# Starting the first attention's steps after 512 of 2048 tokens, with the rest of the token work among its first twelve steps

## The chip, the cores and the metric

The kernel runs on one core of a Trainium2 chip. The metric is device microseconds from launch to end; the kernel before takes 1487.89 us, the median of three runs (1487.07 to 1488.57). Five engines run side by side, each through its own instruction queue in order: PE (matrix multiply, with weight loads shown as PEld), DVE (vector), ACT (scalar), POOL (GpSimd) and SP, which issues most of the DMAs. Engines wait for each other through semaphores.

## The reference, cut to what matters

Two layers over x of 2048 tokens by 128. The change touches the first attention of the first layer only. It has 16 heads of 8 dimensions, and its weights are relu(scores) over their sum:

```python
xn = _layernorm(x, axis=-1)
# first attention, on xn
qkv = (xn @ w_qkv).reshape(Bx, Sx, H, 3 * HD)
q, k, v = jnp.split(qkv, 3, axis=-1)          # each to (B, H, S, HD), HD = 8
scores = jnp.einsum('bhqd,bhkd->bhqk', q, k) / sqrt(HD)
w = relu(scores)
attn = w / (jnp.sum(w, axis=-1, keepdims=True) + KERN_EPS)
out = jnp.einsum('bhqk,bhkd->bhqd', attn, v)
out = out.transpose(0, 2, 1, 3).reshape(Bx, Sx, D) @ w_out + b_out
y = xn + out
s = (y - mean(y)) * rsqrt(var(y) + LN_EPS) * gamma + beta
g = silu(routed_block(xn))                     # ranks tokens by a router, treats 255 of them
x = x + s * g                                  # then the second layer
```

## The kernel before, in words

**Program order.** PE, ACT and DVE run in the order in which the program is written (a manual schedule); POOL's and SP's instructions are put in order by a planner that follows dependencies and priorities.

**Prelude.** `begin()` (L795) runs before the attention's steps. The 2048 tokens are four blocks of 512. For each, the generator `normalised(i)` (L764) works in two halves: first statistics (L774 to L777: four BN pairs and a sum on DVE, a square root on ACT), then the reciprocal and four small DVE operations (L779 to L783), four DVE normalisations into `xne` (L785), four PE transposes (L101) and an ACT copy into `xnT` (L103). `keys(i)` (L712) projects block i onto group 0's keys and `queries()` (L721) block 0 onto group 0's queries. Both go through `project` (L700): one matmul of 512 columns, an ACT copy that rounds the result to `high` (fp32r), and a DVE operation (L709) that leaves in each row either the high part or the difference, by the per-partition scalars `low_k` and `low_q` (L137). `values(i)` (L752) makes the values of four 128-token chunks. All four blocks go through all of it before the first step.

**Rows.** fp32 scores are made from two fp32r parts of each operand: a quadrant of 32 partitions holds one head, with four variants (high or low key by high or low query) of its 8 dimensions. Before, the variant is the outer index (rows n*8 + d); `low_k` tests bit 16 and `low_q` bit 8 of the partition number.

**Steps.** 256 steps (L964): 4 query chunks of 512, by 4 groups of 4 heads, by 16 key chunks of 128. `scores(n)` (L818) is four matmuls (L824), one for each head, in four quadrants at once, each into a PSUM bank of tag "s" (6 banks), then four relus, on ACT (L832) or DVE (L834) by the running totals `work.a` and `work.d` (`Work.lesser`, L189). `products` (L837) of two steps earlier is four matmuls (L840) into one accumulator, copied by ACT at the end of a group (`group_out`, L847). After these, a step either does the piece that `due` lists for it, or takes one turn of `others()`: the routed block (router, ranking, its own small attention), then weights and the gated output of finished chunks. The routed block and `spread` share the one PSUM bank of tag "x".

**Other groups' keys and queries.** `all_keys(i)` (L746) and `all_queries(qc)` (L749) project all 16 heads of a block at once through `spread` (L724): a matmul, an ACT copy to `high` (two buffers), a DVE subtraction to `low`, and four stores into DRAM in the order of the variants. `group` (L741) loads 128 rows back with one DMA into `kT` or `qT`. `due` has all_queries(0) at step 1, all_keys(0 to 3) at steps 4, 8, 12 and 16, and the other query chunks at 40, 104 and 168. `read` has the loads of groups 1 to 3.

**The routed block's start.** `routed_block` (L217) loads its weights, sets up constants on POOL (L245 to L271) and yields once; that first turn is taken before `begin()` (L695).

Of the kernel before, what the change touches and what calls it, by code (L numbers as in the profile page):

```python
# [11 lines left out]
F32 = mybir.dt.float32  # L12
# [5 lines left out]
ALU = mybir.AluOpType  # L18
# [4 lines left out]
P = 128  # L23
# [3 lines left out]
NQ = S // 512  # L27
H = 16
HD0 = 8
G = 4  # L30
# [75 lines left out]
def layer0(ctx, tc, a, small, ident, xin, xn1T, row_load, second):  # L106
    nc = tc.nc

    ends, steps, block = ExitStack(), ExitStack(), ExitStack()
    ps = steps.enter_context(tc.tile_pool(name="l0_ps", bufs=1, space=PSUM))  # L110
    dram = ctx.enter_context(tc.tile_pool(name="rb_dram", bufs=2, space=DRAM))
    end = ends.enter_context(tc.tile_pool(name="l0_end", bufs=1, side="right"))
    keep = steps.enter_context(tc.tile_pool(name="l0", bufs=1))


    aw = steps.enter_context(tc.tile_pool(name="aw", bufs=2))
    w_qkv = aw.tile([P, 512], F32, tag="high", name="w_qkv")[:, : 3 * D].rearrange(
        "p (g j t d) -> p g j t d", g=G, j=4, t=3
    )
    nc.scalar.dma_start(  # L120
        out=w_qkv.rearrange("p g j t d -> p (g j t d)"), in_=a["w_qkv"]
    )

    w_k = keep.tile([P, 4, 4, HD0], F32, name="w_k")
    w_q = keep.tile([P, 4, 4, HD0], F32, name="w_q")
    for i in range(4):
        for t, dst in ((1, w_k), (0, w_q)):
            nc.gpsimd.tensor_copy(dst[:, :, i, :], w_qkv[:, 0, :, t, :])
    w_ka = keep.tile([P, H, HD0], F32, name="w_ka")
    w_qa = keep.tile([P, H, HD0], F32, name="w_qa")  # L130
    for t, dst in ((1, w_ka), (0, w_qa)):
# [85 lines left out]
def routed_block(  # L217
# [3 lines left out]
    nc = tc.nc  # L221
# [8 lines left out]
    for t, n in enumerate(("wq", "wk", "wv")):  # L230
# [9 lines left out]
    pos = rb.tile([P, NC], I32, name="r_pos")  # L240
    nc.sync.dma_start(out=pos, in_=a["pos"])


    tok = rb.tile([P, 512], F32, name="tok")
    nc.gpsimd.iota(  # L245
# [6 lines left out]
        out=before, in_=before, pattern=[[-1, P]], compare_op=ALU.is_gt,  # L252
# [12 lines left out]
    nc.gpsimd.tensor_copy(xne[:, :, 130], pos)  # L265

    qk = rb.tile([P, 2 * H, 32], F32, tag="qk_p4", name="qk")
    nc.gpsimd.memset(qk, 0.0)
    v = rb.tile([P, 2, H, 32], F32, name="r_v")
    nc.gpsimd.memset(v, 0.0)  # L270
    nc.gpsimd.memset(v[:, :, :, HD0 : HD0 + 1], 1.0)  # L271
# [408 lines left out]
def relu_attention(  # L680
# [3 lines left out]
    nc = tc.nc  # L684
# [12 lines left out]
    def bank(shape, tag="x"):  # L697
        return ps.tile(shape, F32, tag=tag, bufs=NS if tag == "s" else 1, name="t")

    def project(dst, w, i, low, tag="x"):  # L700

        t = bank([P, 512], tag)
        nc.tensor.matmul(
            t, w.rearrange("p b a d -> p (b a d)"), xnT[:, 512 * i : 512 * i + 512],
            start=True, stop=True,
        )
        high = aw.tile([P, 512], F32R, tag="high", name="high")
        nc.scalar.copy(high, t)
        nc.vector.scalar_tensor_tensor(dst, high, low, t, ALU.mult, ALU.add)  # L709
        work.add(a=0.6, d=0.75)  # L710

    def keys(i):  # L712
        project(kT[:, 0, 512 * i : 512 * i + 512], w_k, i, low_k, "s")

    qTs = {}

    def query_tile(qc, g):
        t = qTs[qc, g] = aw.tile([P, 512], F32R, tag="qT", bufs=3, name=f"qT_{qc}_{g}")
        return t

    def queries():  # L721
        project(query_tile(0, 0), w_q, 0, low_q, "s")

    def spread(w, i, order):  # L724


        t = bank([P, 512])
        nc.tensor.matmul(
            t, w.rearrange("p h d -> p (h d)"), xnT[:, 512 * i : 512 * i + 512],
            start=True, stop=True,  # L730
        )
        parts = [aw.tile([P, 512], F32R, tag=n, name=n) for n in ("high", "low")]
        nc.scalar.copy(parts[0], t)
        nc.vector.scalar_tensor_tensor(parts[1], parts[0], -1.0, t, ALU.mult, ALU.add)
        work.add(a=0.6, d=0.75)
        rows = dram.tile([G, 4, 4, HD0, 512], F32, tag="spread", bufs=8, name="spread")
        for n, x in enumerate(order):
            nc.sync.dma_start(out=rows[:, :, n, :, :], in_=parts[x].bitcast(F32))
        return rows

    def group(rows, g, dst):  # L741
        nc.sync.dma_start(out=dst.bitcast(F32), in_=rows[g].rearrange("j n d q -> (j n d) q"))

    asked, key_rows = {}, {}

    def all_keys(i):  # L746
        key_rows[i] = spread(w_ka, i, (0, 0, 1, 1))

    def all_queries(qc):  # L749
        asked[qc] = spread(w_qa, qc, (0, 1, 0, 1))  # L750

    def values(i):  # L752
        t = bank([P, 4, P], "s")
# [10 lines left out]
    def normalised(i):  # L764
# [27 lines left out]
        )  # L792
        yield

    def begin():  # L795
        parts = [normalised(i) for i in range(NQ)]
        next(parts[0])
        for i in range(NQ):
            if i + 1 < NQ:
                next(parts[i + 1])  # L800
            next(parts[i])
            if i:
                keys(i - 1)
            if i == 1:
                queries()
        values(0)
        keys(NQ - 1)
        for i in range(1, NQ):
            values(i)
        work.a = work.d = 0.0  # L810

# [126 lines left out]
        return [mv[:, i, 0:1] for i in range(n)], [r[:, i : i + 1] for i in range(n)]  # L938

    n_steps = NQ * G * NC  # L940
    due = {1: (all_queries, 0)}
    read = {}
    for i in range(NQ):
        due[4 + 4 * i] = (all_keys, i)
        for g in range(1, G):
            read[8 + 4 * i if g == 1 else 16 * g - 10 + 3 * i] = (g, i)
    for qc in range(1, NQ):
        due[64 * qc - 24] = (all_queries, qc)

# [9 lines left out]
            yield from gated(qc)  # L959

    ends, steps, block = pools
    ready, held, other = set(), [], others()
    begin()
    for n in range(n_steps + 2):  # L964
        if n < n_steps:
            held.append((n, scores(n)))
        if n >= 2:
            m, r = held.pop(0)
            products(m, r)
            if m % 16 == 15:  # L970
                group_out(m // 64, m // 16 % 4)
        if n in due:
            f, *args = due[n]
            f(*args)
        else:
            next(other)
        if n % 16 == 8 and 16 < n + 8 < n_steps:
            qc, g = (n + 8) // 64, (n + 8) // 16 % 4
            group(asked[qc], g, query_tile(qc, g))
# [746 lines left out]
```

## Time and profile before

| what | value |
|---|---|
| median of three runs | 1487.89 us |
| the profiled execution: its own time / its span | 1487.12 / 1485.1 us |
| busy, whole span: PE, DVE, ACT, POOL | 96%, 73%, 65%, 22% |
| mean granted clock of PE | 0.991 |
| first scores of step 0 start | 37.73 us |
| last scores of step 255 start | 500.92 us |
| relus: ACT 620 of mean 625 ns, DVE 404 of mean 684 ns | 326.3 and 261.2 us busy |

The profile is one execution. Busy times are sums over instructions; a span's rate is read better from the starts of successive instructions of one kind, since matmuls overlap in the pipeline. Scores of step n are recognised by L824, products by L840. Up to 37.7 us the engines go through the prelude; the steps follow to about 503 us, and the second layer after that.

### The profile page before, as it was taken

The numbers are of one execution on the slowest core, as the hardware profiler recorded it, in microseconds if no ns is written. First come the engines' busy times: TensorE is split into PE (matmuls) and PEld (weight loads), VectorE is DVE, ScalarE is ACT, GpSimd is POOL, SyncE is SP. The second block draws the span as 40 slices with busy tenths as digits, with TensorE's granted clock in tenths as the row PEclk, the third lists the DMA queues.
The fourth block names the chain that finished last, engine by engine and source line by source line (L and its number), as shares of the span: only waits on it lengthen the run. The fifth ranks groups of instructions, "written<-read, shape, count | busy, mean of one in ns | idle before, by whom it ended". The sixth has DMA issues, their size and how long they took to land.

```text
span 1485.1 us, 27124 instructions
## 1 busy us (share of the span) xinstructions
PE 1431.8 (96%) x10336; PEld 877.3 (59%) x10336; DVE 1079.6 (73%) x1938; ACT 967.2 (65%) x2080; POOL 325.2 (22%) x445
## 2 busy tenths in 40 slices
PE   4999999999999999999999999999999999999997
PEld 2223233332222367777777777777777777777775
DVE  5797878778888667567677667667767766777765
ACT  2787878778878656656556556556656655665663
POOL 1001000050000123322332242242242232252310
PEclk8999999999999999999999999999999999999999
DMA  2621100100200220000010010010001001000000
GB/s 66 186 66 61 32 12 14 49 26 14 60 20 4 79 50 15 15 16 15 21 24 15 15 30 15 15 29 15 15 15 29 15 15 29 15 15 16 15 22 22
DMA packets 28192, 44.70 MB, mean 30 GB/s; under 512 B 5984, under 2 KB 14560, under 8 KB 28064
## 3 DMA queue, kind: packets, MB, share of 16 engines
q1 hardware_dynamic: 27376, 41.94, 11.0%
q8 instruction: 81, 1.33, 0.4%
q0 software_dynamic: 256, 0.79, 0.2%
q14 instruction: 47, 0.39, 0.1%
q10 hardware_dynamic: 432, 0.26, 0.1%
HBM read 14.76 MB, written 10.11 MB: 17 GB/s over the span
## 4 chain that ended last, share of the span: by engine, by line
PE 60%; ACT 2%; DVE 1%; issue 1%; DVEq 0%; ACTq 0%
PE t L1326 18%; PE z L1376 17%; PE t L1556 16%; PE m L1436 2%; PE m L1264 2%; PE m L1229 2%; PE m L1279 2%; PE m L1421 2%; ACT p L1360 1%; ACT pt L1563 1%; PE m L1158 0%; DVE tops L1347 0%; PE m L1176 0%; DVE t L1346 0%; DVE pt L1563 0%
## 5 line engine op out<-in xcount | busy, mean ns | idle before, releaser
L1347 DVE TENSOR_REDUCE tops<-t 128x1 f32<-128x1024 f32 (+4 forms) x320 | 334.6, 1062 | 63.2 <-PE t L1326 56.0
L832 ACT ACTIVATE rt<-t 128x512 f32<-128x512 f32 x620 | 326.3, 625 | 76.1 <-PE t L824 75.0
L1563 ACT COPY pt<-t 128x512 f32<-128x512 f32 (+3 forms) x359 | 163.4, 518 | 266.9 <-PE t L1556 265.8
L1360 ACT ACTIVATE p<-t,tops 128x1024 f32<-128x1024 f32 (+7 forms) x384 | 331.2, 882 | 2.9 <-DVE tops L1347 2.2
L1326 PE MATMUL t<-k,q 128*128 128x512 f32 (+4 forms) x1280 | 316.6, 390 | 7.4 <-ACT p L1360 7.4
L834 DVE TENSOR_SCALAR rt<-t 128x512 f32<-128x512 f32 x404 | 261.2, 684 | 45.4 <-PE t L824 38.6
L840 PE MATMUL t<-rt,va 128*9 128x512 f32 x2048 | 270.3, 601 | 4.2 <-ACT part L856 3.8
L1556 PE MATMUL t<-ident,p 128*128 128x128 f32 x2176 | 270.1, 275 | 3.0 <-ACT x L1250 1.4
L1376 PE MATMUL z<-pt,v 128*64 128x256 f32 (+1 forms) x2304 | 268.3, 374 | 0.5 <-ACT zs L1570 0.5
L1326 PEld LDWEIGHTS t<-k,q 128*128 128x128 f32 x1280 | 218.6, 189 | 79.7 <-issue 36.1
L1556 PEld LDWEIGHTS t<-ident,p 128*128 128x128 f32 x2176 | 244.0, 141 | 25.5 <-ACT pt L1563 2.9
L1376 PEld LDWEIGHTS z<-pt,v 128*64 128x64 f32 x2304 | 151.6, 136 | 86.9 <-issue 21.4
L824 PEld LDWEIGHTS t<-qT,kT 32*128 32x128 f32 x1024 | 64.8, 183 | 189.0 <-ACT rt L832 112.9
L1563 DVE COPY pt<-t 128x512 f32<-128x512 f32 (+3 forms) x289 | 163.5, 605 | 2.6 <-PE z L1376 1.5
L824 PE MATMUL t<-qT,kT 32*128 32x512 f32 x1024 | 157.3, 500 | 4.5 <-DVE rt L834 3.1
L1346 DVE TENSOR_TENSOR t<-t,mask_q 128x128 f32<-128x128 f32 (+1 forms) x192 | 65.0, 339 | 85.8 <-PE t L1326 78.3
L1252 POOL CAST q<-x 64x512 fp32r<-64x512 f32 x60 | 36.8, 613 | 371.7 <-ACT x L1250 338.9
L1360 ACT ACTIVATION_READ_ACCUMULATOR p<-t,tops 128x1 f32 x384 | 84.1, 219 | 0.0
L1426 DVE TENSOR_TENSOR zs<-zs,m 128x512 f32<-128x512 f32 (+1 forms) x49 | 32.7, 676 | 64.3 <-PE m L1421 64.1
L1254 POOL TENSOR_TENSOR k<-x,k 64x512 fp32r<-64x512 f32 x60 | 76.4, 1273 | 4.6
L1254 POOL TENSOR_TENSOR q<-x,q 64x512 fp32r<-64x512 f32 x60 | 76.3, 1272 | 4.6
L840 PEld LDWEIGHTS t<-rt,va 128*9 128x9 f32 x2048 | 30.7, 88 | 69.5 <-issue 61.0
(291 smaller groups left out, 1068.1 us busy)
## 6 DMA issues: line engine op xcount, KB each, us to landing
q<-q SPq DMA_DIRECT2D x64, 256.0 KB
spread<-high SPq DMA_DIRECT2D x16, 256.0 KB
spread<-low SPq DMA_DIRECT2D x16, 256.0 KB
qT<-spread SPq DMA_DIRECT2D x15, 256.0 KB
kT<-spread SPq DMA_DIRECT2D x12, 256.0 KB
xin<-in_x SPq DMA_DIRECT2D x4, 256.0 KB
on<-part SPq DMA_DIRECT2D x64, 16.0 KB
wide<-inverse SPq DMA_DIRECT2D x32, 32.0 KB
```

What stands on the lines that cost most here:

```text
L824: nc.tensor.matmul(t, kT[rows, g, kb * P : (kb + 1) * P], qTs[qc, g][rows, :], start=True, stop=True,)
L832: nc.scalar.activation(rt, t, AF.Relu, scale=scale)
L834: nc.vector.tensor_scalar(rt, t, scale, 0.0, ALU.mult, ALU.max)
L840: nc.tensor.matmul(acc[32 * j : 32 * j + HD0 + 1, :], va[:, kb, 4 * g + j, :], r[j], start=(kb == 0), stop=(kb == NC - 1),)
L1254: nc.gpsimd.tensor_tensor(low, x[half(e), :], high, ALU.subtract)
L1326: nc.tensor.matmul(flat[:, at_x : at_x + y - x], q[:, part, c4 * P : (c4 + 1) * P], k[:, x:y], start=(part == 0), stop=(part == 1),)
L1346: nc.vector.tensor_tensor(last, last, mask, ALU.add)
L1347: nc.vector.tensor_reduce(M[pr, c // 4][:, h, c % 4, es], x, axes, ALU.max, negate=True)
L1360: nc.scalar.activation(dst, x, AF.Exp, bias=M[pr, c // 4][:, h, c % 4, e : e + 1], accum_out=Z[pr, c // 4][:, h, c % 4, e : e + 1],)
L1376: nc.tensor.matmul(l1.z[half(e), slot, lo:2, :], V[pr, h][:, kb, half(e)], pts[e][:, kb, lo:2, :], start=(kb == 0), stop=(kb >= n0 - 1), s ...
L1556: nc.tensor.transpose(t[:, k + b, :], x[lo + b], ident)
L1563: copy(dst, t)
```

## The change

Four things, in one diff.

1. `begin()` does the whole of block 0, and of block 1 the normalisation, and the statistics of block 2: then keys(0), queries() and values(0), and the steps start. What is left goes into `due`: keys(1) at step 0, block 2's second half and block 3's statistics at step 1, values(1), (2) and (3) at steps 3, 6 and 9, block 3's second half at step 4. keys(2) and keys(3) are no longer projected for group 0 alone: all_keys(2) and (3), now at steps 2 and 5, give group 0 its rows too, by DMAs straight from `high` and `low`. all_keys(1), all_queries(0) and all_keys(0) come at 7, 8 and 11. `work.d` starts at 3.0 where both totals started at 0.
2. The DVE half of a projection (the low part, or the choice by row) is returned as a function and called in the next step, after that step's scores and relus; the stores are issued there too.
3. Rows within a quadrant are ordered by dimension first (rows d*4 + n; bits 2 and 1). A spread stores two parts of 128 rows instead of four variants; `group` loads with four DMAs of 32 rows, each to every fourth partition.
4. The routed block's first yield is ahead of its POOL constants and memsets rather than behind them.

The diff, cut:

```diff
-    w_k = keep.tile([P, 4, 4, HD0], F32, name="w_k")
-    w_q = keep.tile([P, 4, 4, HD0], F32, name="w_q")
-    for i in range(4):
-        for t, dst in ((1, w_k), (0, w_q)):
-            nc.gpsimd.tensor_copy(dst[:, :, i, :], w_qkv[:, 0, :, t, :])
+    w_k = keep.tile([P, 4, HD0, 4], F32, name="w_k")
+    w_q = keep.tile([P, 4, HD0, 4], F32, name="w_q")
+    for t, dst in ((1, w_k), (0, w_q)):
+        for i in range(4):
+            nc.gpsimd.tensor_copy(dst[:, :, :, i], w_qkv[:, 0, :, t, :])
...
-    for n, bit in (("k", 16), ("q", 8)):
+    for n, bit in (("k", 2), ("q", 1)):
...
     nc.sync.dma_start(out=pos, in_=a["pos"])
 
+    yield
 
     tok = rb.tile([P, 512], F32, name="tok")
...
-    yield
 
     wrow = rb.tile([P, S], F32, tag="wrow_qkT", name="wrow")
...
-    def project(dst, w, i, low, tag="x"):
-
-        t = bank([P, 512], tag)
+    def project(dst, w, i, low):
+
+        t = bank([P, 512], "s")
...
         nc.scalar.copy(high, t)
-        nc.vector.scalar_tensor_tensor(dst, high, low, t, ALU.mult, ALU.add)
         work.add(a=0.6, d=0.75)
+        return lambda: nc.vector.scalar_tensor_tensor(dst, high, low, t, ALU.mult, ALU.add)
...
         nc.scalar.copy(parts[0], t)
-        nc.vector.scalar_tensor_tensor(parts[1], parts[0], -1.0, t, ALU.mult, ALU.add)
         work.add(a=0.6, d=0.75)
-        rows = dram.tile([G, 4, 4, HD0, 512], F32, tag="spread", bufs=8, name="spread")
+
+        def split():
+            nc.vector.scalar_tensor_tensor(parts[1], parts[0], -1.0, t, ALU.mult, ALU.add)
+            rows = dram.tile([2, P, 512], F32, tag="spread", bufs=8, name="spread")
+            return [p.bitcast(F32) for p in parts], rows
+
+        return split
+
+    def kept(parts, rows):
+        for n, part in enumerate(parts):
+            nc.sync.dma_start(out=rows[n], in_=part)
+
+    def group(parts, order, g, dst):
+
         for n, x in enumerate(order):
-            nc.sync.dma_start(out=rows[:, :, n, :, :], in_=parts[x].bitcast(F32))
-        return rows
-
-    def group(rows, g, dst):
-        nc.sync.dma_start(out=dst.bitcast(F32), in_=rows[g].rearrange("j n d q -> (j n d) q"))
+            nc.sync.dma_start(out=dst.bitcast(F32)[n::4, :], in_=parts[x][32 * g : 32 * g + 32, :])
...
     def all_keys(i):
-        key_rows[i] = spread(w_ka, i, (0, 0, 1, 1))
+        split = spread(w_ka, i)
+
+        def later():
+            parts, rows = split()
+            if i >= 2:
+                key_group(parts, i, 0)
+            kept(parts, rows)
+            key_rows[i] = [rows[n] for n in range(2)]
+
+        return later
...
+    tokens = [normalised(i) for i in range(NQ)]
+
     def begin():
...
+        next(tokens[0])
+        next(tokens[1])
+        next(tokens[0])
+        k = keys(0)
+        next(tokens[1])
+        q = queries()
+        k()
+        next(tokens[2])
+        q()
         values(0)
...
+        work.a, work.d = 0.0, 3.0
+
+    def more_keys():
+        return keys(1)
+
+    def more(i):
+
+        next(tokens[i])
+        work.add(a=0.6, d=2.0)
+        if i + 1 < NQ:
+            next(tokens[i + 1])
+            work.add(a=0.2, d=1.8)
...
-    due = {1: (all_queries, 0)}
-    read = {}
+
+    due = {
+        0: (more_keys,), 1: (more, 2), 2: (all_keys, 2), 3: (more_values, 1), 4: (more, 3),
+        5: (all_keys, 3), 6: (more_values, 2), 7: (all_keys, 1), 8: (all_queries, 0),
+        9: (more_values, 3), 11: (all_keys, 0),
+    }
+    read = {
+        9: (2, 1), 10: (3, 1), 12: (1, 1), 14: (0, 1),
+    }
     for i in range(NQ):
-        due[4 + 4 * i] = (all_keys, i)
-        for g in range(1, G):
-            read[8 + 4 * i if g == 1 else 16 * g - 10 + 3 * i] = (g, i)
+        for g in range(2, G):
+            read[16 * g - 10 + 3 * i] = (i, g)
...
             held.append((n, scores(n)))
+        if later:
+            later()
+            later = None
         if n >= 2:
...
             f, *args = due[n]
-            f(*args)
+            later = f(*args)
...
-        elif n == 5:
-            group(asked[0], 1, query_tile(0, 1))
         if n in read:
-            g, i = read[n]
-            group(key_rows[i], g, kT[:, g, 512 * i : 512 * i + 512])
+            i, g = read[n]
+            key_group(key_rows[i], i, g)
+        if n == 11 or (n > 16 and n % 16 == 8 and n + 8 < n_steps):
+            m = 16 if n == 11 else n + 8
+            qc, g = m // 64, m // 16 % 4
+            group(asked[qc], OF_Q, g, query_tile(qc, g))
```

More of the change, by code (lines that the diff above doesn't have):

```diff
@@ L267, in routed_block @@
     qk = rb.tile([P, 2 * H, 32], F32, tag="qk_p4", name="qk")
+    v = rb.tile([P, 2, H, 32], F32, name="r_v")
     nc.gpsimd.memset(qk, 0.0)
-    v = rb.tile([P, 2, H, 32], F32, name="r_v")
     nc.gpsimd.memset(v, 0.0)
     nc.gpsimd.memset(v[:, :, :, HD0 : HD0 + 1], 1.0)
-    yield
     wrow = rb.tile([P, S], F32, tag="wrow_qkT", name="wrow")
@@ L698, in bank @@
         return ps.tile(shape, F32, tag=tag, bufs=NS if tag == "s" else 1, name="t")
-    def project(dst, w, i, low, tag="x"):
-        t = bank([P, 512], tag)
+    def project(dst, w, i, low):
+        t = bank([P, 512], "s")
         nc.tensor.matmul(
-            t, w.rearrange("p b a d -> p (b a d)"), xnT[:, 512 * i : 512 * i + 512],
+            t, w.rearrange("p a d n -> p (a d n)"), xnT[:, 512 * i : 512 * i + 512],
             start=True, stop=True,
@@ L708, in project @@
         nc.scalar.copy(high, t)
-        nc.vector.scalar_tensor_tensor(dst, high, low, t, ALU.mult, ALU.add)
         work.add(a=0.6, d=0.75)
+        return lambda: nc.vector.scalar_tensor_tensor(dst, high, low, t, ALU.mult, ALU.add)
     def keys(i):
-        project(kT[:, 0, 512 * i : 512 * i + 512], w_k, i, low_k, "s")
+        return project(kT[:, 0, 512 * i : 512 * i + 512], w_k, i, low_k)
     qTs = {}
@@ L721, in queries, with spread @@
     def queries():
-        project(query_tile(0, 0), w_q, 0, low_q, "s")
-    def spread(w, i, order):
+        return project(query_tile(0, 0), w_q, 0, low_q)
+    def spread(w, i):
         t = bank([P, 512])
@@ L733, in spread, with key_group, later @@
         nc.scalar.copy(parts[0], t)
-        nc.vector.scalar_tensor_tensor(parts[1], parts[0], -1.0, t, ALU.mult, ALU.add)
         work.add(a=0.6, d=0.75)
-        rows = dram.tile([G, 4, 4, HD0, 512], F32, tag="spread", bufs=8, name="spread")
+        def split():
[7 more added lines that the diff above has]
+    def group(parts, order, g, dst):
         for n, x in enumerate(order):
-            nc.sync.dma_start(out=rows[:, :, n, :, :], in_=parts[x].bitcast(F32))
-        return rows
-    def group(rows, g, dst):
-        nc.sync.dma_start(out=dst.bitcast(F32), in_=rows[g].rearrange("j n d q -> (j n d) q"))
+            nc.sync.dma_start(out=dst.bitcast(F32)[n::4, :], in_=parts[x][32 * g : 32 * g + 32, :])
+    OF_K, OF_Q = (0, 0, 1, 1), (0, 1, 0, 1)
     asked, key_rows = {}, {}
+    def key_group(parts, i, g):
+        group(parts, OF_K, g, kT[:, g, 512 * i : 512 * i + 512])
     def all_keys(i):
-        key_rows[i] = spread(w_ka, i, (0, 0, 1, 1))
-    def all_queries(qc):
-        asked[qc] = spread(w_qa, qc, (0, 1, 0, 1))
+        split = spread(w_ka, i)
[6 more added lines that the diff above has]
+        return later
+    def all_queries(qc):
+        split = spread(w_qa, qc)
+        def later():
+            parts, rows = split()
+            kept(parts, rows)
+            asked[qc] = [rows[n] for n in range(2)]
+        return later
     def values(i):
@@ L793, in normalised, with more_values @@
         yield
+    tokens = [normalised(i) for i in range(NQ)]
     def begin():
[L796 to L805, printed above, removed]
-        values(0)
[L807 to L810, printed above, removed]
+        next(tokens[0])
[7 more added lines that the diff above has]
+        q()
+        values(0)
+        work.a, work.d = 0.0, 3.0
[7 more added lines that the diff above has]
+            work.add(a=0.2, d=1.8)
+    def more_values(i):
+        values(i)
+        work.add(a=0.6)
     acc = bank([P, 512], "acc")
@@ L961, in relu_attention @@
     ends, steps, block = pools
-    ready, held, other = set(), [], others()
+    ready, held, other, later = set(), [], others(), None
     begin()
@@ L973, in relu_attention @@
             f, *args = due[n]
-            f(*args)
+            later = f(*args)
         else:
             next(other)
-        if n % 16 == 8 and 16 < n + 8 < n_steps:
-            qc, g = (n + 8) // 64, (n + 8) // 16 % 4
-            group(asked[qc], g, query_tile(qc, g))
-        elif n == 5:
-            group(asked[0], 1, query_tile(0, 1))
-        if n in read:
-            g, i = read[n]
-            group(key_rows[i], g, kT[:, g, 512 * i : 512 * i + 512])
+        if n in read:
+            i, g = read[n]
[4 more added lines that the diff above has]
+            group(asked[qc], OF_Q, g, query_tile(qc, g))
         if n >= 2 and (n - 2) % 64 == 6 and n > 64:
```

## The prediction

> **What bounds it now.** I read the busy slices first (PE at 9 tenths in all but the first and last slice), then the same by stages, then the timeline of the first 130 us.
>
> ```profile
> 0.00:20.00 20.00, 5.81 (x12) 2.56 (x12) 12.43 (x53) 3.78 (x8) 7.09 (x34) 1.00 0.52 122
> 20.00:37.70 17.70, 10.48 (x46) 6.96 (x46) 8.32 (x31) 5.36 (x10) 0.00 (x0) 0.71 0.00 0
> 37.70:63.05 25.35, 25.00 (x159) 7.24 (x158) 17.28 (x31) 17.04 (x32) 0.21 (x1) 1.00 0.57 176
> 63.05:116.26 53.21, 49.58 (x328) 12.93 (x328) 52.81 (x111) 47.90 (x97) 0.00 (x0) 0.94 0.31 93
> ```
>
> Columns: length, then busy PE, PEld, DVE, ACT, POOL, the granted clock, DMA. The prelude leaves every engine idle half the time: it is a chain. Steps 0 to 11 (37.7 to 63.05) are PE's. The ranking phase (63 to 116) fills DVE and nearly ACT, and there PE waits. Later steps are PE's again:
>
> ```profile
> 455.87 0.66 PE L101 MATMUL t<-ident,y 128*128 128x128 f32 x4
> 456.45 0.51 PE L824 MATMUL t<-qT,kT 32*128 32x512 f32 x4
> 456.89 1.05 PE L840 MATMUL t<-rt,va 128*9 128x512 f32 x8
> 457.87 0.51 PE L824 MATMUL t<-qT,kT 32*128 32x512 f32 x4
> 56.52 1.12 PE L728 MATMUL t<-xnT,w_ka 128*128 128x512 f32 x2
> 57.58 0.51 PE L824 MATMUL t<-qT,kT 32*128 32x512 f32 x4
> 34.96 2.84 PE L756 MATMUL t<-w_v,xnT 128*128 128x128 f32 x24
> ```
>
> Start to start, scores take 0.44 us, products 0.98, so a bare step 1.42; four transposes 0.58; a 512-column projection 1.06; three values() 2.77 (34.96 to the first scores at 37.73). Steps 0 to 11 then sum to 12 x 1.41, less two absent products, plus 7 projections (four router, three spreads) and 4 x 0.58: 24.7 of the 25.3 us measured; 0.6 was lost.
>
> **The change, part by part.** The sum stands on the profiled execution: span 1485.1, its own time 1487.12. The median of the runs, 1487.89, is 0.77 above it; I apply the difference to the median.
>
> *First scores earlier.* Until DVE ends the first normalisation (12.0) nothing changes; the first xnT block is copied at 13.2. PE then runs keys(0) to 15.1 (1.91 for such a projection at 16.17), the second block's transposes to 16.1, queries to 18.0, values(0) to 18.9 or 19.8 by its clock. DVE: keys' difference 16.6, third block's statistics 18.6 (1.9 as at 21.16), query difference 19.45. First scores at 19.5 to 19.9; I take 19.6: **-18.1**.
>
> *Work moved into PE-bound steps.* keys(1) 1.06, two sets of transposes 1.2, three values() 2.77: **+5.0**. keys(2) and keys(3) as own projections vanish with the prelude; group 0 of blocks 2 and 3 comes from their all_keys spreads, which ran anyway.
>
> *Waits in steps 0 to 4.* A normalisation's second half is one DVE chain of 2.1 us:
>
> ```profile
> 22.95 0.17 DVE L779 RECIPROCAL y<-y 128x4 f32<-128x4 f32 x1
> 23.95 1.11 DVE L785 TENSOR_SCALAR xne<-xin,ln_mv,ln_r 128x128 f32<-128x128 f32 x4
> ```
>
> The starting d=3.0 sends step 0's four relus to ACT (0.52 each, 20.2 to 22.3); behind them is the high copy of keys(1) (to 22.9), behind that its DVE difference (23.7), behind that block 2's second half (25.8). PE's transposes stand in its queue before scores(2), so they end at 26.0: PE did 2.5 us of work since 19.6, 3.9 lost. Then ACT's square root of block 3 waits for DVE's statistics (28.0) with step 2's four relus behind it; scores(3) need two of their banks: 0.6. Scores(4) lose 0.4 the same way. Block 3's transposes wait for DVE from 33.2 to 34.35 and are paced to 35.3: 1.5. Together **+6.4**, less the 0.6 that the old steps lost: **+5.8** (0 if this all overlaps, 8 if each link slips by a relu).
>
> *Later splits.* The low part is now computed after the next step's scores and relus, on DVE behind up to two relus (1.29), while the next user of the one "x" bank waits on PE. Products end 1.41 after scores; the split at 0.5+1.29+0.7 = 2.5: 1.1 lost after steps 7 and 11, 0.8 after 104 and 168. Step 40 falls in the ranking phase, free. **+3.8** (0 with no DVE relu in those steps, 5 with both always).
>
> *Ranking phase.* Others get 11 of the first 12 steps taken away instead of 3, so ranking starts near step 19 rather than 11, on DVE that bounds it either way. One spread (0.69 DVE, 0.59 ACT) and one part copy fewer fall in it. Before, a relu on DVE queued behind counts there stopped PE 2.64, 1.70 and 1.70 us (93.0, 95.6, 98.1). Bounds -4 (most of that gone) and +2; I take **-1.0**, nearest the saved ACT and DVE rows. The routed block ends about six steps later; but the last steps before 503 are bare 1.41 us steps waiting for nothing else, so it stays inside: 0. Without that slack each lost turn would cost about a step, 1.4.
>
> *Half clock.*
>
> ```profile
> 92.00:94.00 2.00, 0.96 (x7) 0.42 (x11) 2.00 (x6) 0.08 (x1) 0.00 (x0) 0.50 0.00 0
> 93.76 1.89 PE L840 MATMUL t<-rt,va 128*9 128x512 f32 x8
> 98.71 1.05 PE L840 MATMUL t<-rt,va 128*9 128x512 f32 x8
> ```
>
> After PE's 2.3 us pause at 90.7 the clock fell to 0.50 until about 98.5, and products took 1.89 instead of 1.05. My wait before 25.0 is 2.7 us, so I expect the same around 24 to 30, mostly under waits counted already: **+0.5** (0 to 5). [...]
>
> *Transfers.* Two stores for four per spread, but four 32-row loads for one: SP issues between steps 9 and 14 are 20 loads x 0.43 and 4 stores x 0.6, 11 us in some 13.
>
> ```profile
> 50.55 1.78 SPq L738 DMA_DIRECT2D spread<-low  x2
> 55.77 1.28 SPq L742 DMA_DIRECT2D kT<-spread  x3
> ```
>
> Loads used to follow the last store by 3.4 us with 1 MB stored. Block 0's group-1 rows: split at 56, stores issued by 57.2, loads 59 to 62, wanted by step 16 at 63.6; formerly asked at step 8. The direct loads for group 0 have 6 steps. **+0.3** (0 to 3: half the 1 MB wait, or all of it plus a queued store). Row order inside a quadrant changes no matmul shape, low_k and low_q stay per-partition scalars, and w_k's strided copies are needed 8 us after they end (0; cover is DVE's first normalisation).
>
> *POOL's memsets after the yield.*
>
> ```profile
> 8.65 1.39 DVE L779 RECIPROCAL y<-y 128x4 f32<-128x4 f32 x1
> 9.73 0.19 POOL L425 MEMSET inv<- 128x1 f32 x4
> 9.87 0.14 POOL L271 MEMSET r_v<- 128x32 f32 x1
> ```
>
> That reciprocal takes 0.17 elsewhere; it ended as the L270 memset did, and ln_v at 6.29 (0.83 for 0.17) likewise: 1.9 us on the chain. But L425, some 60 turns later in the program, ran before L271: POOL isn't kept in program order, so I expect the memsets where they were: 0 (to -1.9). [...]
>
> Sum: -18.1 +5.0 +5.8 +3.8 -1.0 +0.5 +0.3 = **-3.7**; 1487.9 - 3.7 = **1484.2**.
>
> **Rivals.** *Waits overlap (1478).* Splits find DVE free (-3.8+0.5) and ranking loses its three PE stops (-3): -10. For it: ACT and DVE are busy only 17 of 25 us in the old steps 0 to 11. Against: in-order queues, each link above has its predecessor in front. *Eaten whole (1487.5).* all_queries(0) reuses the "high" buffer whose six transfers were issued only around 40 to 44; its ACT copy at 46.2 waits, relus behind it, and step 16 waits for rows: 1.5 to 2 each. For it: SP's 11 of 13 us. Against: half the stored bytes. *Half clock stays (1492).* PE's pauses at 24 and 34 hold the clock at 0.50 from 24 past step 8. Each step then costs 0.84 (products) + 0.29 (scores 0.80 for 0.51) more, its projection another 1; seven steps give 13 less some 5 hidden in waits: +8. It decides from two low stretches of 6.8 us on; one is covered. For it: the row at 93.76. Against: steps 5 to 11 keep PE full, and it rose at 98.5 after five such microseconds. *The change not doing what it says*: scores(0) waiting for something later than block 1; I see nothing in its operands.
>
> **Chances.** Forecast (1481 to 1487) 0.40, overlap 0.32, eaten 0.13, half clock 0.15. This kernel's measurement tells about 0.2%, 3 us, from no change, so faster means below 1484.9: 0.32 and 0.25 of the forecast's, 0.57; same: 0.15 of the forecast's and 0.11, 0.26; slower: 0.15 and 0.02, 0.17. The range 1477 to 1491 leaves out the overlap's lower tail and the half clock's upper half; the forecast's own is 1481 to 1487.
>
> **What would show it.** First L824 near 19.6; PE waiting for DVE xne ahead of two L101 groups inside the steps, some 2.7 and 1.1 us; L834 or the low part ahead of PE's x-bank users by about 1 us after steps 7 and 11; clock at 0.50 once before 35; step 19 near 70 (77.0 before); last step rigidly shifted. I am wrong if step 5 starts before 33 or after 38, if rank's stops vanish, or if the first reciprocal is short.

## The result, and the profile after

| | before | after |
|---|---|---|
| median, run side by side (12 runs each) | 1487.16 us | 1486.68 us (1486.13 to 1488.17) |
| ratio after / before, 95% interval | | 0.9995 [0.9987, 1.0004] |
| the profiled execution: own time / span | 1487.12 / 1485.1 us | 1487.31 / 1485.2 us |
| first scores | 37.73 us | 19.02 us |
| last scores (step 255) | 500.92 us | 500.48 us |

No change that can be told. The steps start 18.7 us earlier, and 0.4 us of that is left at the last step. The time lies in the forecast's range, which was wide; the likeliest case, faster by 3.7 us, did not come.

After, by stages (columns: stretch, length, busy PE, PEld, DVE, ACT, POOL, granted clock, DMA share, GB/s):

```profile
0.00:19.02 19.02, 6.54 (x21) 3.86 (x22) 13.06 (x54) 4.75 (x9) 7.06 (x34) 1.00 0.47 128
19.02:53.91 34.89, 29.60 (x175) 10.20 (x175) 20.16 (x50) 21.58 (x43) 0.00 (x0) 0.95 0.34 104
53.91:72.00 18.09, 16.99 (x123) 5.16 (x122) 11.51 (x23) 10.92 (x21) 0.21 (x1) 1.00 0.36 101
72.00:123.85 51.85, 47.43 (x310) 12.54 (x314) 51.38 (x107) 46.64 (x95) 0.00 (x0) 0.97 0.18 51
123.85:500.48 376.63, 369.62 (x2939) 117.21 (x2939) 300.86 (x593) 296.39 (x581) 39.85 (x73) 0.99 0.09 23
```

The second row is steps 0 to 11: 34.9 us where they took 25.3, PE idle for 5.3 of them and the clock at 0.95. The fourth is the ranking, from the first count of the routed block to the sum of the counts: DVE is busy 51.38 of 51.85 us. PE's timeline after, its waits in brackets:

```profile
19.02 0.51 PE L865 MATMUL t<-qT,kT 32*128 32x512 f32 x4 [0.62 <-DVE qT L710]
...
20.51 1.16 PE L865 MATMUL t<-qT,kT 32*128 32x512 f32 x4
24.28 1.15 PE L101 MATMUL t<-ident,xne 128*128 128x128 f32 x4 [2.61 <-DVE xne L812]
...
26.09 1.72 PE L881 MATMUL t<-rt,va 128*9 128x512 f32 x8
...
29.23 1.05 PE L881 MATMUL t<-rt,va 128*9 128x512 f32 x8
...
34.44 1.10 PE L101 MATMUL t<-ident,xne 128*128 128x128 f32 x4 [1.66 <-DVE xne L812]
...
45.42 1.12 PE L727 MATMUL t<-xnT,w_qa 128*128 128x512 f32 x2 [1.02 <-DVE low L736]
...
56.49 1.13 PE L281 MATMUL x<-xnT,rwb 128*128 128x512 f32 x2 [1.10 <-DVE low L736]
...
102.24 0.53 PE L865 MATMUL t<-qT,kT 32*128 32x512 f32 x4 [3.64 <-DVE rt L875]
...
115.06 1.12 PE L727 MATMUL t<-xnT,w_qa 128*128 128x512 f32 x2
```

Both waits for a normalisation and both for a late split are there. So is a low clock (products 1.72 us at 26.09, 1.05 at 29.23), and in the ranking PE still stops for a relu on DVE. That relu is queued behind counts, in DVE's timeline:

```profile
100.03 1.55 DVE L303 TENSOR_SCALAR_CACHE_REDUCE junk<-wrow,wcol 128x1280 bf16<-128x1280 f32 x1
101.50 0.08 DVE L303 DVE_READ_ACCUMULATOR junk<-wrow,wcol 128x1 f32 x1
101.50 0.69 DVE L875 TENSOR_SCALAR rt<-t 128x512 f32<-128x512 f32 x1
```

In the prelude the memsets stand where they stood, and the reciprocal beside them is still long (1.38 us):

```profile
8.36 1.38 DVE L806 RECIPROCAL y<-y 128x4 f32<-128x4 f32 x1
...
8.54 0.94 POOL L271 MEMSET r_v<- 128x1024 f32 x1
9.44 0.19 POOL L425 MEMSET inv<- 128x1 f32 x4
9.57 0.14 POOL L272 MEMSET r_v<- 128x32 f32 x1
```

**The lead, by stages.** Because the routed block's turns fall on other steps, step numbers alone mislead. I compare at the same turn: a step ahead is worth 1.412 us of PE (a bare step: before, the scores of fifteen in a row run from 461.03 to 482.22), a spread already done 1.06. The ranking runs from step 12.21 (63.58 us) to 38.33 (116.26) before, and from 20.08 (72.00) to 45.46 (123.85) after. Spreads in it are, before, those of steps 12 and 16, with step 40's behind it:

```profile
64.47 1.13 PE L728 MATMUL t<-xnT,w_ka 128*128 128x512 f32 x2
...
72.08 1.13 PE L728 MATMUL t<-xnT,w_ka 128*128 128x512 f32 x2
...
122.01 1.13 PE L728 MATMUL t<-xnT,w_qa 128*128 128x512 f32 x2
```

After, step 40's alone lies in it (115.06 above). At its start the lead is 7.87 steps x 1.412 + 2.12 for the spreads of steps 12 and 16, less 8.42 us: 4.81. At its end it is 7.13 x 1.412 + 1.06 for the spread of step 40, less 7.59 us: 3.54.

| kernel | lead at step 0 | ranking's start | spreads in it | its end | step 255 | median | ratio to before [95%] |
|---|---|---|---|---|---|---|---|
| after | 18.71 | 4.81 | 1 | 3.54 | 0.44 | 1486.68 | 0.9995 [0.9987, 1.0004] |
| e1_order | 18.34 | 4.67 | 1 | 2.77 | 0.90 | 1486.37 | 0.9987 [0.9979, 0.9996] |
| e2_split | 18.39 | 3.72 | 1 | 1.69 | -0.35 | 1487.13 | 0.9991 [0.9982, 0.9999] |
| e3_pool | 19.77 | 5.89 | 1 | 4.61 | 1.45 | 1486.35 | 0.9990 [0.9982, 0.9999] |
| e4_idle | -0.72 | -2.03 | 1 | -3.36 | -1.98 | 1490.46 | 1.0017 [1.0008, 1.0026] |
| e5_hold10 | 18.23 | -3.39 | 1 | -5.24 | -4.21 | 1489.37 | 1.0009 [1.0001, 1.0018] |
| e5_hold4 | 18.22 | -0.22 | 1 | -1.86 | -4.92 | 1491.06 | 1.0023 [1.0015, 1.0032] |
| e6_rows | -1.00 | -0.99 | 2 | -0.99 | -0.81 | 1487.78 | 1.0002 [0.9993, 1.0011] |
| e7_d0 | 18.03 | 1.84 | 1 | 0.33 | 1.38 | 1486.55 | 0.9994 [0.9985, 1.0004] |
| e8_early | 18.16 | 5.89 | 0 | 3.39 | -1.08 | 1488.92 | 1.0001 [0.9992, 1.0010] |
| e9_early_pool | 19.77 | 7.93 | 0 | 5.53 | 3.70 | 1485.15 | 0.9986 [0.9978, 0.9995] |
| e10_warm | 18.21 | 5.14 | 1 | 3.87 | 0.49 | 1485.93 | 0.9989 [0.9980, 0.9998] |
| e11_all | 19.85 | 9.05 | 0 | 6.66 | 3.10 | 1485.59 | 0.9983 [0.9974, 0.9992] |

(Leads from one profiled execution each; before, beside them, had medians of 1487.2 to 1488.3.) Most of what follows rests on this table.

### The profile page after: what moved, and what is told of

It reads as the page before. It is cut to its first block, busy times and chain, and to the rows that moved or that the text cites. A ratio compares the mean times of both kernels' runs of the same rounds, so it can differ in the third digit from the quotient of the medians.

```text
span 1485.2 us, 27215 instructions
## 1 busy us (share of the span) xinstructions
PE 1431.3 (96%) x10332; PEld 876.5 (59%) x10332; DVE 1076.1 (72%) x1932; ACT 968.1 (65%) x2082; POOL 324.2 (22%) x445
## 3 DMA queue, kind: packets, MB, share of 16 engines
q8 instruction: 81, 1.33, 0.4%
## 4 chain that ended last, share of the span: by engine, by line
PE 59%; DVE 2%; ACT 2%; issue 1%; DVEq 0%; ACTq 0%
PE t L1375 17%; PE z L1425 16%; PE t L1605 15%; PE m L1485 2%; PE m L1313 2%; PE m L1278 2%; PE m L1328 2%; PE m L1470 2%; ACT p L1409 1%; DVE tops L1396 1%; ACT pt L1612 0%; PE m L1207 0%; DVE t L1395 0%; DVE pt L1612 0%; PE m L1225 0%
## 5 line engine op out<-in xcount | busy, mean ns | idle before, releaser
L865 PE MATMUL t<-qT,kT 32*128 32x512 f32 x1024 | 160.8, 500 | 7.1 <-DVE rt L875 4.3
```

What stands on the lines that cost most here:

```text
L865: nc.tensor.matmul(t, kT[rows, g, kb * P : (kb + 1) * P], qTs[qc, g][rows, :], start=True, stop=True,)
```

## The experiments

Theory A, at first: the change's own pieces and waits eat the gain. Rival B: the gain is real, and lost where the routed block's turns now fall on other steps.

**e1_order: the order of the first pieces.**

```diff
-        0: (more_keys,), 1: (more, 2), 2: (all_keys, 2), 3: (more_values, 1), 4: (more, 3),
+        0: (more, 2), 1: (more_keys,), 2: (all_keys, 2), 3: (more_values, 1), 4: (more, 3),
```

> The changed kernel with two pieces swapped: block 2's second half of the normalisation at step 0, keys(1) at step 1. Theory A (the wait of 3.9 us ahead of step 2 stands because the DVE half of block 2 is queued behind keys(1)'s chain through ACT): PE's wait ahead of the first L101 group inside the steps falls from 2.6 to under 1 us, step 5 starts near 33.2 instead of 35.47, and the end moves by most of that: 1484.4 (1483.5 to 1485.5). Rival B (what is gained in the first steps is lost again once the routed block's turns fall on other steps and the low clock on other instructions): step 5 earlier all the same, but the end within 0.7 us of 1486.7.

PE's timeline with the two pieces swapped:

```profile
20.75 1.01 PE L101 MATMUL t<-ident,xne 128*128 128x128 f32 x4 [0.84 <-DVE xne L812]
...
23.95 1.46 PE L865 MATMUL t<-qT,kT 32*128 32x512 f32 x3 [0.27 <-ACT rt L873]
...
34.58 1.10 PE L101 MATMUL t<-ident,xne 128*128 128x128 f32 x4 [1.66 <-DVE xne L812]
```

The wait of 2.61 us shrank to 0.84, but step 5 began at 35.61 (35.47 after). ACT's square root of block 3 waits for DVE's statistics, step 1's four relus stand behind it, and step 2's scores need their banks: 2.16 us from the first of them to the next products, 0.73 after. The low clock, now from 26.51 to 29.93, fell on a PE that had work: the projection at 26.31 took 1.92 us for 1.12, the scores at 28.16 0.80 for 0.51. So the order moves the loss: from its own first scores to step 5 it saved 0.2 us. The end is 0.13% below before, by an interval that overlaps after's.

**e2_split: the split in its own step.**

```diff
             later = f(*args)
+            if f in (all_keys, all_queries):
+                later = later()
```

> The changed kernel with the low part of every spread computed at once, in the same step as its matmul, as before the change. Theory A (a later split holds the one x bank): the waits of PE for the low part ahead of steps 9 and 13 (1.02 and 1.10 us) vanish, those after 104 and 168 too, 2 to 3.8 us in all: 1483.5 to 1485. Rival B (the split at once makes DVE wait for ACT's copy with relus behind it, and scores then wait for banks): within 0.7 us of 1486.7, or slower.

PE's idle time between steps 5 and 19 fell from 2.12 us to 0.00: the late split costs what the forecast gave it at steps 7 and 11. The time did not follow. In this execution the low clock took 5.1 us in steps 0 to 19 (length times one minus the granted clock, summed over slices of 1.7 us) where it took 1.7 after.

**e3_pool: POOL's work held back.** The token count and the clearing of `qk` and `v` get an input from the second block's normalised tokens, by a one-column copy.

```diff
+    nc.gpsimd.tensor_copy(tok[:, 0:1], xne[:, 7, 0:1])
...
+    for t in (qk, v.rearrange("p b h d -> p (b h) d")):
+        nc.gpsimd.tensor_copy(t[:, 0, 0:1], xne[:, 7, 0:1])
+        nc.gpsimd.memset(t, 0.0)
```

> The changed kernel with POOL's iota into tok and its memsets of qk and v made to follow the second block's normalisation (each preceded by a copy of one column that reads it). If POOL's memsets are what stretches the first square root's sum and the reciprocal (0.77 and 1.38 us for 0.17 elsewhere): those fall to about 0.35 and 0.2, first scores start near 17.4 instead of 19.02, and the end moves to 1485.1 (1484.3 to 1486). If the stretch has another cause, the reciprocal stays at 1.4 us and the time at 1486.7. Rival B of the other runs: first scores near 17.4, end within 0.7 us of 1486.7.

DVE's and POOL's timelines with that:

```profile
8.56 0.17 DVE L808 RECIPROCAL y<-y 128x4 f32<-128x4 f32 x1
```

```profile
14.25 0.95 POOL L273 MEMSET qk<- 128x1024 f32 x1
15.14 0.95 POOL L273 MEMSET r_v<- 128x1024 f32 x1
```

The reciprocal takes 0.17 us instead of 1.38 (before, it ended at 10.04, the memset of L270 at 9.78 and that of L271 at 10.01), and the first scores come at 17.96, 1.06 earlier. That 1.06 is still there at the ranking's start (5.89 against 4.81), at its end (4.61 against 3.54) and at step 255 (1.45 against 0.44): a gain made ahead of the ranking does pass through it.

**e4_idle: the shift alone.** The kernel before, with the turns of steps 2 to 9 left out, so that everything in the routed block comes six steps later (all of it is still done).

```diff
-        else:
+        elif not 2 <= n < 10:
             next(other)
```

> The kernel before, with nothing of the change but one: the turns of the routed block at steps 2 to 9 are left out, six in all, so that from step 17 on every turn falls on the same step as in the changed kernel (the turns are all taken later, nothing of the computation is left out). Rival B (the shift of the turns against steps and group ends by six costs the 3 us that the changed kernel lost after step 70): 1489 to 1490.5, 1.5 to 3 us slower than before. Theory A (the loss comes from the change's own pieces): 1487.2, within 0.7 us of before.

Slower: 1.0017 [1.0008, 1.0026], some 2.5 us, without one of the change's pieces. Its window over its ranking, and that of the kernel before over its own (after's is the fourth row further up):

```profile
79.23:130.60 51.37, 47.72 (x308) 12.86 (x310) 50.86 (x106) 45.41 (x92) 0.00 (x0) 0.93 0.13 40
```

```profile
63.58:116.26 52.68, 49.05 (x320) 12.65 (x323) 52.31 (x109) 47.70 (x96) 0.00 (x0) 0.94 0.31 93
```

DVE is busy all but 0.4 to 0.5 us in every one. It sets the length of the ranking, and PE gets done in it what it can. Before, that was 26.12 steps and the two spreads of steps 12 and 16; in this kernel 25.00 steps and one spread, that of step 40, the other two having fallen ahead of it. 26.12 x 1.412 + 2.12 = 39.0 us of PE work against 25.00 x 1.412 + 1.06 = 36.4, in 1.31 us less: 1.33 lost, as the table has it. That is not the whole of its 2.5 us: its lead was -2.03 before the ranking began, and why is not traced.

**e5_hold10 and e5_hold4: turns held ahead of the ranking.** After, with the turns of steps 12 to 21, and of 12 to 15, held.

```diff
-        else:
+        elif not 12 <= n < 22:
             next(other)
```

> The changed kernel with the routed block's turns left out at steps 12 to 21, ten in all (taken later, nothing of the computation is left out), so that they stand 16 steps later than in the kernel before: on the same place within a group of 16 steps. Rival B, in the form that the place within a group matters (part copies and group loads at fixed steps): the 3 us come back, 1484 (1483 to 1485.2) against 1486.7 for the changed kernel. In the form that any new meeting of turns, relu shares and low clock gives another sum: anywhere from 1484.5 to 1489. Theory A (the change's own pieces): 1486.7, within 0.7.

> The same with four turns left out at steps 12 to 15, ten later than in the kernel before, on another place within the group. Place within a group: no recovery, 1486 to 1488.5. Any new meeting: 1484.5 to 1489, not the same as with ten. Theory A: 1486.7, within 0.7.

1489.37 us, ratio 1.0009 [1.0001, 1.0018], and 1491.06, 1.0023 [1.0015, 1.0032]: four held steps cost more than ten, which neither theory had. Steps 0 to 255 took 4.2 and 4.9 us longer than after, and the low clock 5.1 us more in each (11.9 against 6.8). So these two say more on the clock than on turns. They are the same program up to step 12 and start it 0.01 us apart, yet the ten-step kernel's windows read

```profile
26.00:29.00 3.00, 3.00 (x13) 0.76 (x14) 1.07 (x6) 2.31 (x6) 0.00 (x0) 0.50 0.00 0
...
38.00:41.00 3.00, 3.00 (x10) 0.50 (x2) 0.60 (x1) 1.45 (x3) 0.00 (x0) 0.50 0.17 49
```

and the four-step kernel's

```profile
26.00:29.00 3.00, 3.00 (x14) 0.58 (x14) 1.07 (x7) 2.31 (x6) 0.00 (x0) 0.66 0.00 0
...
38.00:41.00 3.00, 3.00 (x26) 1.33 (x24) 1.29 (x2) 2.22 (x5) 0.00 (x0) 1.00 0.13 29
```

Step 6 started at 41.37 in the first and 38.45 in the second: 2.9 us between equal programs, which differ in the clock (the third column from the end). It was low from 24.07 to 30.90 and from 37.73 to 41.14 in the first, from 24.62 to 28.04 in the second.

**e6_rows: the rows alone.** The kernel before with rows by dimension, two stores and four loads a group.

```diff
-    w_k = keep.tile([P, 4, 4, HD0], F32, name="w_k")
+    w_k = keep.tile([P, 4, HD0, 4], F32, name="w_k")
...
+        for n, x in enumerate(order):
+            nc.sync.dma_start(out=dst.bitcast(F32)[n::4, :], in_=parts[x][32 * g : 32 * g + 32, :])
```

> The kernel before with the rows by dimension alone: two stores for a spread instead of four, four loads of 32 rows instead of one of 128; prelude, due times and splits as before. My term for the transfers was 0.3 us and all of it in the new schedule: within 0.7 us of before, last scores at the same time to 0.5 us. If the four loads or the stride of four partitions cost by themselves (or fewer stored bytes help): 1 us or more either way.

Nothing: 1.0002 [0.9993, 1.0011]. Its steps are 1.0 us late from the first scores on, and stay so through the ranking, whose loss is 0.0: the spreads of steps 12 and 16 still lie in it.

**e7_d0: the relus of step 0.**

```diff
-        work.a, work.d = 0.0, 3.0
+        work.a = work.d = 0.0
```

> The changed kernel with work.d starting at 0 instead of 3.0, so that DVE takes relus of step 0. Two relus on DVE let ACT reach the copy of keys(1) about 1 us earlier, and block 2's half with it: step 2 at 24.5 instead of 25.36, and if that lasts to the end 0.7 us faster (1485.5 to 1486.5). If the order in the first steps is bound elsewhere (block 3's statistics ahead of ACT's square root, then step 3), step 5 stays at 35.5 and the time at 1486.7, within 0.5.

Step 2 started at 26.35 (25.36 after) and step 5 at 37.20 (35.47), so the head start of 3.0 is worth having; the end is the same, 0.9994. It got 1.05 us back after the ranking (0.33 to 1.38); what gave it back is not shown. The mean granted clock of the execution was 0.993, where after's was 0.994.

**e8_early: the turns put back.** After, with six turns taken beside pieces.

```diff
             f, *args = due[n]
+            if n in (0, 1, 4):
+                next(other)
             later = f(*args)
+            if n in (3, 6, 9):
+                next(other)
```

> The kernel after, with one turn of the routed block taken beside the piece in each of steps 0, 1, 3, 4, 6 and 9, so that from step 17 on every turn stands in the same step as in the kernel before. Theory A (the change's own pieces cost it: what the first steps must do for normalisation, keys and values is too much): the six turns only come on top in the steps that are already the longest, the lead at step 19 falls from 6.6 to under 4 us, and the end is where it was, 1486 to 1488. Theory B (the lead was real and was lost because the routed block's turns fell six steps later, on other instructions): the lead from step 17 on is 3.5 to 5 us, stays so through the ranking, the exponentials and the gates, and the time is 1482 to 1484.5, ratio 0.996 to 0.998. A lead that is there at step 30 and gone by step 150 again speaks against B as I have it.

B fell here. With every turn back in its old step the profiled lead goes from 5.89 to 3.39 in the ranking, a loss of 2.5 where the kernel after lost 1.3 (no spread lies in this one's), and then to -1.08. What the turns gain is ahead of the ranking: they fill PE's waits (1.82 and 0.62 us for 2.61 and 1.66).

**e9_early_pool: the same with POOL held.** The two edits together.

> The same six turns, and GpSimd's token count and the clearing of the routed block's queries, keys and values held until the second 512 tokens are normalised. Theory A: as the kernel after with that hold alone, 1486 to 1487. Theory B: the two gains add, one us below the kernel with the six turns alone, 1481 to 1484, ratio 0.995 to 0.9975.

Faster than before, by 0.14%: 0.9986 [0.9978, 0.9995]. Its window over the ranking, and that of the kernel with the turns alone:

```profile
60.84:110.89 50.05, 44.79 (x292) 11.69 (x290) 49.58 (x104) 44.96 (x91) 0.00 (x0) 0.93 0.18 53
```

```profile
62.87:112.92 50.05, 46.04 (x292) 11.66 (x291) 49.58 (x104) 44.62 (x90) 0.00 (x0) 0.90 0.19 53
```

Equal to 0.01 us, though the clock was 0.93 in one and 0.90 in the other and PE's busy time differs by 1.25: the low clock cost nothing here, where DVE sets the pace (busy 49.58 of 50.05 us in both). Both do some 24 steps and no spread in it, and lose 2.4 and 2.5. This kernel's waits of PE (us in total, times, longest) also show two late splits that cost nothing in the trace after, at steps 40 and 104:

```profile
PE x L343 <- DVE low L738: 1.1, 1, 1.1
...
PE x L558 <- DVE low L738: 1.0, 1, 1.0
```

**e10_warm: the clock kept up.** Matmuls whose result nobody reads, in PE's two long waits.

```diff
     def more(i):

+        t = bank([P, 512])
+        for _ in range(4 - i):
+            nc.tensor.matmul(
+                t, w_q.rearrange("p a d n -> p (a d n)"), xnT[:, 0:512], start=True, stop=True,
+            )
         next(tokens[i])
```

> The kernel after, with two matmuls of 1.12 us whose result nobody reads in TensorE's wait of 2.6 us ahead of the third block's transposes, and one in its wait of 1.7 us ahead of the fourth's. Theory A (pauses that lower the clock are a real part of the first steps' cost): the granted clock in 23 to 29 us is 0.95 or more instead of 0.68 and 0.75, the products of step 0 take 1.0 to 1.1 us instead of 1.72, step 5 starts 0.7 to 1.2 us earlier against step 0, and the time is at most 1 us lower, 1485.5 to 1486.5. Theory B (the lead is lost later, whatever it is at step 5): the first steps as under A, but the end is that of the kernel after within its scatter, ratio 0.999 to 1.000. If the clock is as low as before, the pause isn't what lowers it.

The windows after, and with the extra matmuls:

```profile
23.00:26.00 3.00, 1.72 (x8) 1.01 (x8) 2.75 (x14) 1.11 (x3) 0.00 (x0) 0.68 0.00 0
26.00:29.00 3.00, 3.00 (x18) 0.62 (x14) 0.64 (x4) 2.30 (x7) 0.00 (x0) 0.75 0.00 0
```

```profile
23.00:26.00 3.00, 2.29 (x11) 0.94 (x9) 2.79 (x13) 1.25 (x4) 0.00 (x0) 1.00 0.00 0
26.00:29.00 3.00, 3.00 (x22) 0.88 (x22) 1.32 (x8) 2.17 (x6) 0.00 (x0) 1.00 0.00 0
```

Filling the pauses with work for nothing keeps the clock up here, at 1.00 where it was 0.68 and 0.75: steps 0 to 5 took 15.61 us for 16.45, and the ratio is 0.9989 [0.9980, 0.9998]. The lead at step 255 is hardly more than after's, 0.49, but this execution began its steps 0.5 us later.

**e11_all: all together.** Six turns, POOL held, and one such matmul (under `if i == 2`).

> The six turns back in their old steps, GpSimd's clearing held back, and one matmul of 1.12 us whose result nobody reads ahead of the third block's transposes, where TensorE still waited 1.8 us and the clock fell for one stretch of 3.41 us. If each such stretch costs its half, 1.7 us, and the gains add: no granted clock below 0.95 before step 19, step 5 some 1.7 us earlier against step 0 than with the six turns and the hold alone (18.1 us from step 0 to step 5 there), and a median of 1483 to 1484, ratio 0.9970 to 0.9980. If the lead is lost later whatever it is at step 5: 1484.5 to 1486, ratio 0.9985 to 0.9995. If the clock falls all the same, the matmul comes too late to shorten the pause.

Its PE timeline, where the clock fell before:

```profile
23.14 1.12 PE L847 MATMUL t<-xnT,w_q 128*128 128x512 f32 x2 [0.92 <-ACT wrow L284]
24.10 1.06 PE L101 MATMUL t<-ident,xne 128*128 128x128 f32 x4
25.09 0.50 PE L872 MATMUL t<-qT,kT 32*128 32x512 f32 x4
25.52 1.05 PE L888 MATMUL t<-rt,va 128*9 128x512 f32 x8
```

Products at 1.05 us, where the clock of the kernel without the matmul stood at 0.50 from 24.10 to 27.50, and steps 0 to 5 in 17.08 us for 18.11: 1.0 gained, not 1.7. The extra matmul cost nothing (the transposes start 6.2 us after step 0 in both); but the four transposes take 0.99 us to the next scores here and only 1.18 at the low clock, since DVE's four normalisations, 1.12 us in all, pace them either way. The lead is 9.05 at the ranking's start and 3.10 at step 255; 1485.59 us, 0.9983 [0.9974, 0.9992]. It is the fastest by ratio, not to be told from the kernel without the matmul (0.9986).

## Why the forecast missed, step by step

**Up to the ranking it held.** Step 5 came at 35.47 (33 to 38), step 19 at 70.47 (near 70). The forecast had -18.1 and +13.8 (5.0 + 5.8 + 2.2 + 0.5 + 0.3), a lead of 4.3; measured 4.81. The terms: first scores -18.71 for -18.1. Waits and splits of steps 0 to 11: PE's idle time 6.39 less the old 0.34, so 6.0 for 8.0; block 2's transposes waited 2.61 (my 3.9 was elapsed time less PE's work; counted so it was 3.8, 19.02 to 25.36 less 2.5), block 3's 1.66 for 1.5, the splits 1.02 and 1.10 for 1.1 each, and the 0.6 and 0.4 ahead of scores(3) and scores(4) don't show as waits. Moved work was too small: four transposes that follow DVE's normalisations one by one (1.12 us for the four) take 1.03 us to the next scores (34.44 to 35.47), not the 0.58 read where their input was ready, and a values() 1.09 (30.21 to 31.30), not 0.92; with keys(1) that is 6.4 for 5.0. Low clock 1.7 (3.40 us at 0.50, from 24.10 to 27.50) for 0.5. Transfers 0 for 0.3: PE waits for no DMA in the steps. POOL's memsets stayed, as read from L425 and L271.

**The step that failed is the ranking phase, "-1.0".** DVE's share of it was right: the stretch fell from 52.68 to 51.85, by 0.83. What was left out is that PE works in that stretch for nothing extra. Before, it did 26.12 steps and two spreads there; after, 25.38 steps and one. 39.0 us of PE work against 36.9, in 0.83 less: **+1.3**, where -1.0 stood (my bounds were -4 and +2). I had counted rightly that one spread fewer falls in it, and its DVE and ACT work as saved, but not PE's work on it and on its step as lost.

The kernels order by the spreads that are left in the ranking. With two (before, e6_rows) they lose nothing there; with one, in nine kernels, 1.3 to 2.0 us; with none, in the three with the turns put back, 2.4 to 2.5. The ranking lasts 52.68, 51.4 to 52.5, and 50.05 us. So a spread with its step takes 2.47 us of PE (1.06 + 1.412) where PE is the bound, and lengthens the ranking by some 1.3. The kernel with the shift alone loses 1.33 with none of the change's pieces. (e1_order and e2_split lose 1.9 and 2.0; why 0.6 more than after, I did not settle.) "It stays inside: 0", for the routed block's later end, was the wrong question: its place relative to the spreads counts.

**After the ranking** the forecast lost 1.6 to the splits of steps 104 and 168; measured 3.10 (3.54 to 0.44), from elsewhere. In the trace after, PE waits for no low part there. The low clock takes 3.4 us in steps 50 to 78 (187.95 to 194.78 at 0.50) where it took 1.7 before (183.78 to 187.2), and PE is idle 0.75 us longer in steps 145 to 255; the other 0.6 is not traced. Much of this is the execution: e8_early and e9_early_pool, with the same turns, lose 4.5 and 1.8 us there; in the first the low clock took 3.4 us of it (180.7 to 187.6 at 0.50), and the mean granted clock of the two executions was 0.990 and 0.994. From step 255 to the end it is another 0.54. So the sum: lead 0.5 better than forecast at the ranking, then 2.3 worse through it, 1.5 and 0.5 later, 3.8 in all: nothing left.

**The rivals.** "Eaten whole" has the right time and the wrong mechanism: no wait for the high buffer shows. "Overlap" needed the ranking's stops to go; one of 3.64 us came instead of one of 2.33 and some short ones. (The 1.70 us that I read as stops at 95.6 and 98.1 are none: PE was busy for all of both, at a granted clock of 0.50 and 0.89.) "Half clock stays" is real in single executions, as the two held kernels show, but the most that I saw ahead of step 12 was one low stretch of 6.8 us and one of 3.4, in e5_hold10 and e2_split, and not its seven steps.

What stays open: no run moved one spread back into the ranking by itself; that one is worth some 1.2 us there comes from comparing kernels that differ in more. What the leads do after the ranking is explained only in part. And since the low clock differs between executions of one kernel (mean granted clock 0.991 to 0.996 in the twelve of e9_early_pool), the profiled leads at step 255 carry some 2 us of it, an estimate from the 2.9 us between the two held kernels; the ratios don't hang on a single execution.

## What to carry to other kernels

Find the stretches in which another engine sets the pace, and count what the bound engine does there: work moved out of them costs its full time in the new place (2.47 us here for a spread and its step) and may shorten them by less (1.3). Compare two schedules at the same piece of work, not at the same step number. And price a piece that another engine feeds bit by bit by a row where it is fed so (four transposes here: 1.03 us, and 0.58 where their input was ready).

## What the hardware showed that I had not expected

In these traces the granted clock falls to 0.50 and rises to 1.00 on a grid. Found in narrow windows, the edges lie at 23.38, 33.64, 91.65, 98.47, 183.78 and 187.2 us before, and at 24.10, 27.50, 102.6, 187.95 and 194.78 after. All the low stretches whose two edges I located are one, two or three times 3.41 us long, and the gaps between edges multiples too (58.01 is 17 times, 85.31 and 85.35 are 25). So each low stretch, at a clock of 0.50, can cost up to half of 3.41 us, or of a multiple, where PE is the bound. Measured: the two held kernels, equal so far, had lost 5.1 and 1.7 us to it by step 6 and were 2.9 us apart; in e11_all one stretch of 3.41 us less gained 1.0. That the grid's place against the program is what makes one execution differ from another is argued from this, not shown. The executions of after lie within 2.0 us, those of e9_early_pool between 1482.85 and 1488.40.

What makes it fall is open. In the 3.41 us ahead of the fall PE was busy for 0.00 us (23.38 before), 2.47 (91.65), 2.35 (183.78), 0.98 (24.10 after, the scores from 20.69 to 21.67), 0.36 (102.6) and 3.01 (187.95); in e1_order, ahead of 26.51, it was idle for only 0.27. The fall at 91.65 came inside PE's pause from 90.70 to 93.03, not after it as the forecast has it.
